# W_out's load moved to SyncE's queue, the temperature steps held until the first group's evictions, and a new set of planner ranks

## Chip, cores and metric

The kernel runs on one core of one Trainium2 chip. The metric is the device time of one execution in microseconds (us). The input is 32 sequences of 512 tokens with 256 features, all in f32.

## The reference, cut to what matters

Two blocks follow each other, each with a layer norm ahead of it and a residual sum behind it.

```
x = x + attention(layernorm(x))
    q     = tanh(x W_charge + b);  phi_c = mags * q^(0..4)
    shell = normalised(x W_shell + b);  phi_s = cos, sin(shell omega + bias)
    phi   = (phi_c outer phi_s) W_combine
    logits = phi phi^T * exp(-0.03 |i - j|) / (softplus(log_temp) + 0.1), causal
    out   = softmax(logits) (x W_v + b_v) W_out + b_out
x = x + slots(layernorm(x))
    route = gelu([x, slot mean] w1 + b1) w2 + b2, divided by (|tau| + 0.1)
    alpha = softmax over the 8 largest of 64, zero elsewhere
    gi    = alpha^T x / sum(alpha);  h = GRU(gi, slot state)
    out   = alpha (h wv + bv) wo + bo
```

## The kernel before, in words

The 32 sequences are worked on in 16 groups of two (group g from 0 to 15). A group goes through these stages, named by the tiles that TensorE (PE) writes:

- `pta` (first two groups): x is transposed on PE and copied to `xT` by ScalarE (ACT). Later groups load x a second time in blocks (`xb`, by SyncE's queue, SP) and transpose them on VectorE (DVE).
- `pf` (L959, eight tiles a group): x times the joined weights `wf`. DVE evicts each tile to `sv` (L972), with the layer norm applied. It needs `lna`, which GpSimd (POOL) makes from DVE's `bna` statistics.
- `ptq` (L1018) and `pts` (L1089): the charges (`qrep`, by POOL) and the shells (`shn`, by DVE) turned. ACT follows with `qs` and `shT`. `pp` (L1106) then gives the angles; ACT, DVE (`turn`), ACT's Sin and DVE's products make `tp`.
- `pph` (L1164): `tp` times W_combine. DVE multiplies it by the decays `dec_q` and `dec_k` into `phi` (L1179).
- `pl` (L1221): logits. DVE masks them and takes the lowest (`lg`, L1250), ACT takes the exponential (`pr`, L1262). `ptp` (L1299) turns the weights, ACT copies them (`prT`, L1317), `po` (L1305) multiplies by the values in `sv`, and DVE adds to x (L1334).
- second norm, then `xm` goes to DRAM and back (`xd`, `xmb`) and is transposed by DVE; in the last two groups PE does it (`ptb`).
- `ph` (L1431), `prr`, `prt`: the router; DVE takes the eight largest (`top`). `psi` (L1543), `pt_gi`, `prz`, `pn`, `pt_hn`, `pv`, `py` (L1704): the slots, the GRU and the way back. The result is stored by SP.

Weights are prepared once. `value_and_out` is called twice: for W_v and W_out (pair 0) and for wv and wo (pair 1). It loads the first matrix, the second, a bias `bv` and a bias `bo`, each on the queue that `engs` names; DVE centres the first matrix (pair 0 only, L432 to L435) and spreads `bv` over a tile (`spread`, L469); PE multiplies them (`pw` L446, `pb` L478); DVE copies the products into `wf` or `wov`. In pair 0 the first matrix is loaded by SP, the second by ACT's queue, the biases by POOL's.

The softmax temperature is made in three steps: `scalars_1` on ACT (two Abs, two Exp, the second of which makes `dec_k`), `scalars_2` on DVE (`sa`, `tau`, `rtau`), an Ln on ACT with a table load of its own, and `scalars_3` on DVE, which scales `dec_q`. The four reciprocals of `decays` (L643) wait for the first group's eight evictions.

The order of the work is not written by hand. Every piece is a `Step` with an engine, a cost, the steps that it comes after, and the buffers that it uses. `Plan.order()` places one step after another: of those that could start earliest, the one with the lowest rank. A step without a rank of its own gets one:

```
at = (1.0 - LATE) * s.at + LATE * (longest - s.tail)
delay, late = DELAY[s.stage]
s.rank = s.g * STRIDE + at + delay + late * max(0, s.g - last + 3)
```

HOP is what a step on another engine adds in the plan, TABLE and SWITCH are added to the rank of a step that needs another ACT table or another tiling of PE. Each engine then runs its instructions strictly in the order in which they were placed, and SP issues its DMAs in that order too.

Of the kernel before, what the change touches and what calls it, by code (L numbers as in the profile page):

```python
# [11 lines left out]
AF = mybir.ActivationFunctionType  # L12
# [25 lines left out]
DECAY = 0.3 / 10.0  # L38
# [33 lines left out]
}  # L72


HOP = 0.21
TABLE = 1.28
SWITCH = 4.13
STRIDE = 29.1
LATE = 0.69

DELAY = {
    "setup": (0.0, 0.0),
    "load": (-39.8, 3.7),
    "tokens": (0.2, -3.0),
    "angles": (-18.5, -12.2),
    "phi": (8.4, 6.8),
    "weights": (14.1, -12.0),
    "values": (5.1, -15.9),
    "normal": (-0.8, 5.2),
    "router": (-1.4, -7.2),  # L90
    "taken": (1.6, -23.5),
    "gru": (16.3, 6.1),
    "given": (-12.8, -6.4),
}

SPARE = 3
# [22 lines left out]
class Plan:  # L119
# [8 lines left out]
    def add(  # L128
        self,
        eng,  # L130
        cost,
        emit,
        after=(),
        uses=(),
        table=None,
        land=0.0,
        rank=None,
        spare=0,
        split=None,
    ):  # L140
        s = Step(eng, cost, emit, [a for a in after if a], list(uses), rank, table, land)
        s.spare, s.split = spare, split
        s.g, s.stage = self.group, self.stage
        for u in s.uses:
            u.users += 1
        for a in s.after:
            a.next.append(s)
        s.waits = len(s.after)
        self.steps.append(s)
        return s  # L150
# [95 lines left out]
def block_kernel(ctx: ExitStack, tc: tile.TileContext, a: dict, out: bass.AP):  # L246
    nc = tc.nc
# [24 lines left out]
    add = plan.add  # L272
# [79 lines left out]
    dec_k = const("dec_k", [P, T])  # L352
# [29 lines left out]
    def make_ident():  # L382
# [20 lines left out]
        rank=-40.0,  # L403
# [9 lines left out]
    def value_and_out(wv_ap, bv_ap, wo_t_ap, bo_ap, w_dst, b_dst, n, centred, engs, rank):  # L413

        at = 2 * n
        wv = part(at, 0, [P, KD, D])
        wo_t = part(at, KD * D, [P, KD, D])
        bv_rep = part(at, 2 * KD * D, [P, KD, P])
        bo = part(at, 2 * KD * D + KD * P, [P, D])
        of = wv.of  # L420
        bv = const(f"bv{n}", [P, KD])
        mean = const(f"wv_mean{n}", [P, KD])
        land = 3.5 if centred else None
        l_wv = load(engs[0], wv, rows(wv_ap), 256, rank=rank, land=land)
        l_wo = load(engs[1], wo_t, rows(wo_t_ap), 256, rank=rank, land=land)
        l_bv = load(engs[2], bv, bv_ap.rearrange("(k p) -> p k", p=P), 8, rank=rank)
        l_bo = load(engs[2], bo, bo_ap.partition_broadcast(P), 128, rank=rank)
        last = l_wv
        if centred:

            def centre():
                nc.vector.tensor_reduce(mean, wv(), AX.X, ALU.add)  # L432
                nc.vector.tensor_scalar(mean, mean, 1.0 / D, None, ALU.mult)
                for k in range(KD):
                    nc.vector.tensor_scalar(  # L435
                        wv()[:, k, :], wv()[:, k, :], mean[:, k : k + 1], None, ALU.subtract
                    )

            last = add("DVE", 1.6, centre, [l_wv], of, rank=rank)
        done, made = [], []  # L440
        for m in range(KD):
            pw = bank(f"pw{n}_{m}")

            def project(m=m, pw=pw):
                for k in range(KD):
                    nc.tensor.matmul(  # L446
                        pw()[:, 0:D],
                        wv()[:, k, m * P : (m + 1) * P],
                        wo_t()[:, k, :],
                        start=(k == 0),  # L450
                        stop=(k == KD - 1),
                    )

            s = add("PE", 1.6, project, [last, l_wo], [pw] + of, rank=rank)
            made.append(s)
            done.append(
                add(
                    "DVE",
                    0.42,
                    lambda m=m, pw=pw: nc.vector.tensor_copy(w_dst[:, m, :], pw()[:, 0:D]),  # L460
                    [s],
                    [pw],
                    rank=rank,
                )
            )

        def spread():
            for k in range(KD):
                nc.vector.tensor_scalar(  # L469
                    bv_rep()[:, k, :], onesP, bv[:, k : k + 1], None, ALU.mult  # L470
                )

        s = add("DVE", 0.5, spread, [l_bv, s_ones], of, rank=rank)
        pb = bank(f"pb{n}")

        def project_bias():
            for k in range(KD):
                nc.tensor.matmul(  # L478
                    pb()[:, 0:D],
                    bv_rep()[:, k, :],  # L480
                    wo_t()[:, k, :],
                    start=(k == 0),
                    stop=(k == KD - 1),
                )

        s = add("PE", 1.6, project_bias, [s, l_wo], [pb] + of, rank=rank)
        done.append(
            add(
                "DVE",
                0.42,  # L490
                lambda: nc.vector.tensor_tensor(b_dst, pb()[:, 0:D], bo(), ALU.add),
                [s, l_bo],
                [pb] + of,
                rank=rank,
            )
        )
        return done, made
# [7 lines left out]
        bias_f[:, C_V:NF],  # L505
        0,
        True,
        ("SP", "ACT", "POOL"),
        -40.0,
    )  # L510
    l_bsh = [
# [15 lines left out]
    s = add("PE", 0.8, mean_shell, l_sh + [s_ones] + s_wv_pe, [pm], rank=-38.0)  # L527
# [5 lines left out]
    for q in range(P // SQ):  # L533
        for k in range(KD):
# [8 lines left out]
                    rank=2.0,  # L543
                    land=4.0,
# [7 lines left out]
    for bb in range(GB):  # L552
        r = slice(bb * SHELL, (bb + 1) * SHELL)
        for h in range(2):
# [14 lines left out]
                rank=-15.0,  # L569
                land=5.0,  # L570
# [20 lines left out]
    sa = const("sa", [P, 1])  # L591
# [4 lines left out]
    df = part(0, 2 * KD * D + KD * P + D, [P, T])  # L596
    l_lt = load("SP", lt, a["log_temp"].partition_broadcast(P), 1, rank=-12.0)
    l_tau = load("SP", tau, a["tau"].partition_broadcast(P), 1, rank=-12.0)
# [10 lines left out]
    s_df = add("DVE", 0.42, lambda: nc.vector.tensor_copy(df(), di()), [s_di], [di] + df.of, rank=4.0)  # L609
# [3 lines left out]
    def scalars_1():  # L613
        nc.scalar.activation(sa, lt, AF.Abs)
        nc.scalar.activation(tau, tau, AF.Abs)
        nc.scalar.activation(sa, sa, AF.Exp, scale=-1.0)
        nc.scalar.activation(dec_k, df(), AF.Exp, scale=DECAY)

    def scalars_2():
        nc.vector.tensor_scalar(sa, sa, 1.0, None, ALU.add)  # L620
# [6 lines left out]
        nc.vector.reciprocal(rtemp, sb)  # L627
        nc.vector.tensor_scalar(dec_q, dec_q, rtemp, -1.0, ALU.mult, ALU.mult)

    s = add("ACT", 1.4, scalars_1, [l_lt, l_tau, s_df], df.of, table="exp", rank=4.0)  # L630
    s_exp = s
    s = add("DVE", 0.6, scalars_2, [s], rank=5.0)
    s_tau = s
    s = add("ACT", 1.5, lambda: nc.scalar.activation(sa, sa, AF.Ln), [s], table="ln", rank=5.0)
    s_sb = s

    def decays(after):

        s_rec = [
            add(  # L640
                "DVE",
                0.85,
                lambda c=c: nc.vector.reciprocal(  # L643
                    dec_q[:, c * P : (c + 1) * P], dec_k[:, c * P : (c + 1) * P]
                ),
                [s_exp] + after,
                rank=9.0,
            )
            for c in range(NT)
        ]  # L650
        s_dec.append(add("DVE", 1.0, scalars_3, [s_sb] + s_rec, rank=10.0))

    s_dec = []


    def make_mask():
# [18 lines left out]
        rank=-5.0,  # L675
# [12 lines left out]
            rank=30.0,  # L688
# [28 lines left out]
    s = add("PE", 0.3, hs_transposed, [s_hs, s_ident], [pt_hs], rank=41.0)  # L717
# [10 lines left out]
    def mean_hidden():  # L728
# [5 lines left out]
    s = add("PE", 0.8, mean_hidden, [s_hst, l_w1s], [pb1] + w1s.of, rank=42.0)  # L734
# [6 lines left out]
        rank=42.0,  # L741
# [11 lines left out]
    for lo, n in ((0, 2 * D), (2 * D, D)):  # L753
# [26 lines left out]
        s = add("PE", 2 * n / 300.0, hidden, [s_hst, l_whh], [pg] + hs_t.of + whh.of, rank=70.0)  # L780
# [566 lines left out]
    def router(g, s_x, ln):  # L1347
# [6 lines left out]
        for tiles in ((0, 1), (2,), (3,)):  # L1354
            c = slice(tiles[0], tiles[-1] + 1)
            s = add(
                "POOL",
                0.25,
                lambda c=c: nc.gpsimd.tensor_scalar(  # L1359
                    ln()[:, 2, :, c], ln()[:, 0, :, c], -1.0 / D, None, ALU.mult  # L1360
                ),
                [s_x[bb * NT + i] for bb in range(GB) for i in tiles],
                [ln],
            )
# [59 lines left out]
        for bb in range(GB):  # L1424
# [10 lines left out]
            s = add("PE", 1.78, hidden, done + w1_done, [dst, ph, h_t])  # L1435
# [22 lines left out]
        def routes_turned():  # L1458
# [5 lines left out]
        s = add("PE", 1.01, route, s_h + [l_w2], h_ts + [prr, rl_t], split="128x64")  # L1464
        s = add(
            "ACT",
            0.6,
            lambda: nc.scalar.activation(rl_t(), prr(), AF.Identity, bias=b2),
            [s] + l_b2,
            [prr, rl_t],  # L1470
        )
        s = add("PE", 0.44, routes_turned, [s], [rl_t, prt, rl])
# [9 lines left out]
        for t in range(GT):  # L1482
# [17 lines left out]
        s = add(  # L1500
            "ACT",
            0.68,
            lambda: nc.scalar.activation(rl(), rl(), AF.Exp, scale=rtau),
            [s, s_tau],
            [rl],
            "exp",
        )
# [225 lines left out]
    for g in range(NG):  # L1733
# [10 lines left out]
        sv, s_sv, phi, s_phi = features(g)  # L1744
# [66 lines left out]
```

## Time and profile before

| what | us |
|---|---|
| runs of the kernel, three | 692.91, 693.23, 696.05 |
| median | 693.23 |
| the profiled execution's own time | 696.3 |
| its span, first to last instruction | 694.5 |
| PE busy in that span | 664.7 (96%) |
| DVE busy | 581.4 (84%) |
| ACT busy | 454.2 (65%) |
| POOL busy | 214.0 (31%) |
| first matmul starts | 10.78 |
| last matmul ends | 688.5 |

The three engines DVE, ACT and POOL work beside PE; a wait of theirs counts only where PE ends up waiting too. PE's busy time is the sum over its matmuls, and what is left of the span is PE's idle time at the start, between stages and behind the last matmul. The granted clock in the page's PEclk row is PE's own; where it is below full speed, the same matmul takes longer.

### The profile page before, as it was taken

What the parts mean: (1) busy time and instruction counts of PE and PEld (TensorE: products, weight loads), DVE (VectorE), ACT (ScalarE), POOL (GpSimd) and SP (SyncE); (2) the same over time, 40 slices, a digit from 0 to 9 for tenths busy, and PEclk for the clock granted to TensorE, in tenths of its full rate; (3) what the DMA queues carried; (4) which work ended last, traced back from release to release, by engine and by line L of the source; (5) the groups of instructions that cost most, each with busy time, mean ns of one, the idle gap of its engine ahead of it and who ended that gap; (6) DMA issues with size and microseconds to landing.
All of it is one profiled execution on the core that took longest, in us unless ns stands there. A gap on an engine that the chain in (4) does not pass through costs nothing.

```text
span 694.5 us, 12285 instructions
## 1 busy us (share of the span) xinstructions
PE 664.7 (96%) x3946; PEld 457.7 (66%) x3946; DVE 581.4 (84%) x1812; ACT 454.2 (65%) x1064; POOL 214.0 (31%) x400
## 2 busy tenths in 40 slices
PE   3979999999999999999999999999999999999885
PEld 3747666667666666767666666666766676678453
DVE  3987878799898989989897988989898968878586
ACT  1446676848585866758495775758676677486731
POOL 3550524133150613324061422406151233212200
PEclk9999999999999999999999999999999999999989
DMA  6672732445544444444535353543543433301004
GB/s 179 165 204 68 205 100 73 111 141 130 154 115 130 150 114 161 101 143 128 175 93 149 125 122 135 139 152 96 148 132 82 161 82 87 97 1 62 0 13 170
DMA packets 174255, 83.25 MB, mean 120 GB/s; under 512 B 123664, under 2 KB 173392, under 8 KB 174192
## 3 DMA queue, kind: packets, MB, share of 16 engines
q1 hardware_dynamic: 172880, 81.95, 41.8%
q8 instruction: 31, 0.51, 0.3%
q10 hardware_dynamic: 1104, 0.36, 0.2%
q0 software_dynamic: 208, 0.17, 0.2%
q14 instruction: 32, 0.26, 0.1%
HBM read 50.67 MB, written 31.46 MB: 118 GB/s over the span
## 4 chain that ended last, share of the span: by engine, by line
PE 89%; DVE 4%; DMA 2%; ACT 2%; issue 1%; POOL 0%; ACTq 0%; DVEq 0%; SPq 0%
PE po L1305 20%; PE pf L959 19%; PE ph L1431 7%; PE pl L1221 5%; PE pph L1164 5%; PE ptp L1299 5%; PE psi L1543 5%; PE py L1704 4%; PE prz L1596 4%; PE pn L1596 2%; PE pv L1684 2%; PE prr L1454 2%; PE pta L1667 1%; PE pp L1106 1%; DMA setup<-in_W_out_t_dram 1%; DMA wih<-in_gru_wih_t_dram 1%
## 5 line engine op out<-in xcount | busy, mean ns | idle before, releaser
L1305 PE MATMUL po<-sv,prT 128*128 128x256 f32 x640 | 151.7, 381 | 0.8 <-ACT prT L1317 0.8
L1305 PEld LDWEIGHTS po<-sv,prT 128*128 128x128 f32 x640 | 115.5, 189 | 24.2 <-issue 8.6
L959 PE MATMUL pf<-wfb,xT 128*128 128x321 f32 x448 | 125.6, 436 | 0.0
L959 PEld LDWEIGHTS pf<-wfb,xT 128*128 128x128 f32 x448 | 83.5, 189 | 39.7 <-DVE top L1485 3.5
L1371 ACT ACTIVATE xm<-x,lnb 128x256 f32<-128x256 f32 x128 | 63.9, 502 | 61.7 <-POOL lnb L1359 61.6
L1359 POOL TENSOR_SCALAR lnb<-lnb 128x2 f32<-128x2 f32 (+1 forms) x48 | 20.8, 434 | 266.7 <-DVE x L1334 264.4
L1334 DVE SCALAR_TENSOR_TENSOR x<-po,den,x 128x256 f32<-128x256 f32 x128 | 57.9, 479 | 27.1 <-PE po L1305 26.6
L1262 ACT ACTIVATE pr<-lg,nm 128x512 f32<-128x512 f32 (+3 forms) x128 | 70.8, 557 | 4.9 <-DVE nm L1250 4.0
L972 DVE SCALAR_TENSOR_TENSOR sv<-pf,lna,bias_f 128x321 f32<-128x321 f32 x128 | 64.7, 537 | 5.7 <-PE pf L959 5.1
L1401 ACT ACTIVATE xm<-x,lnb 128x256 f32<-128x256 f32 x112 | 56.9, 589 | 7.8 <-POOL lnb L1387 7.8
L1250 DVE CUSTOM_DVE_ANT_0 lg<-pl,mask 128x512 f32<-128x512 f32 (+3 forms) x128 | 55.6, 479 | 1.6 <-PE pl L1221 1.3
L1718 DVE TENSOR_TENSOR x<-py,x 128x512 f32<-128x512 f32 x64 | 39.8, 683 | 17.4 <-PE py L1704 17.3
L1431 PE MATMUL ph<-xmT,w1b 128*128 128x512 f32 x112 | 52.7, 594 | 0.0
L1317 ACT COPY prT<-ptp 128x384 f32<-128x384 f32 (+1 forms) x96 | 46.1, 516 | 5.4 <-PE ptp L1299 5.2
L800 DVE BATCH_NORM_STATS2 bna<-x 128x6 f32<-128x256 f32 x128 | 49.4, 413 | 0.0
L1299 PE MATMUL ptp<-ident,pr 128*128 128x128 f32 x320 | 45.8, 275 | 0.0
L1221 PE MATMUL pl<-phi 64*128 64x256 f32 (+1 forms) x384 | 43.8, 358 | 0.2 <-DVE phi L1179 0.2
L1299 PEld LDWEIGHTS ptp<-ident,pr 128*128 128x128 f32 x320 | 36.5, 141 | 9.3 <-issue 6.8
L1164 PE MATMUL pph<-tp,wc 64*64 64x256 f32 x640 | 39.8, 392 | 0.8 <-DVE tp L1152 0.8
L1152 DVE TENSOR_TENSOR tp<-tp,qs 128x1024 f32<-128x1024 f32 x32 | 38.7, 1211 | 2.1 <-ACT tp L1138 1.9
L1221 PEld LDWEIGHTS pl<-phi 64*128 64x128 f32 x384 | 30.5, 186 | 11.1 <-issue 7.2
L929 DVE STREAM_TRANSPOSE xT<-xb 128x512 f32<-128x512 f32 x56 | 36.6, 685 | 0.0
(174 smaller groups left out, 1241.6 us busy)
## 6 DMA issues: line engine op xcount, KB each, us to landing
x<-in_x_dram SPq DMA_DIRECT2D x32, 512.0 KB, 4.6
out_dram<-x SPq DMA_DIRECT2D x64, 256.0 KB, 2.5
xb<-in_x_dram SPq DMA_DIRECT2D x112, 128.0 KB, 2.8
xd<-xm SPq DMA_DIRECT2D x28, 512.0 KB, 2.9
xmb<-xd SPq DMA_DIRECT2D x112, 128.0 KB, 2.7
setup<-in_gru_whh_t_dram SPq DMA_DIRECT2D x1, 768.0 KB, 4.6
wih<-in_gru_wih_t_dram SPq DMA_DIRECT2D x1, 768.0 KB, 10.6
wfb<-wf SPq DMA_DIRECT2D x8, 40.1 KB, 3.4
```

What stands on the lines that cost most here:

```text
L959: nc.tensor.matmul(pf()[:, 0:NF], tile_()[:, k, c * P : (c + 1) * P], w[:, k, :], start=(k == 0), stop=(k == KD - 1),)
L972: lambda t=t, pf=pf: nc.vector.scalar_tensor_tensor(sv()[:, t, :], pf()[:, 0:NF], ln()[:, 1, t : t + 1], bias_f, ALU.mult, ALU.add,),
L1164: nc.tensor.matmul(phs[h]()[bb * COMB : (bb + 1) * COMB, 0:HT], wc[r, m, :], tp()[r, m, bb * HT : (bb + 1) * HT], start=(m == 0), stop=(m ...
L1221: nc.tensor.matmul(pls[bb]()[:, off[i] + lo : off[i] + lo + w], phi()[r, 0, q : q + P], phi()[r, 1, k : k + w], start=True, stop=True,)
L1250: nc.vector.tensor_tensor_reduce(out=lg()[:, c], in0=pls[bb]()[:, c], in1=mask[:, T - w : T], scale=1.0, scalar=TOP, op0=ALU.add, op1=ALU.min,
L1262: nc.scalar.activation(pr()[:, c], lg()[:, c], AF.Exp, bias=nm(), scale=-1.0, accum_out=den()[:, tiles.index(i), bb : bb + 1],)
L1299: nc.tensor.transpose(pt()[:, j : j + P], prs[bb]()[:, j : j + P], ident)
L1305: nc.tensor.matmul(po()[:, d * D : (d + 1) * D], pr_t()[:, lo : lo + P], sv()[:, bb * NT + j, C_V:NF], start=(j == 0), stop=(j == i),)
L1334: nc.vector.scalar_tensor_tensor(xt()[:, t, :], po()[:, d * D : (d + 1) * D], den()[:, d, bb : bb + 1], xt()[:, t, :], ALU.mult, ALU.add, ...
L1371: lambda bb=bb, i=i: nc.scalar.activation(xm()[:, bb * NT + i, 0:D], xt()[:, bb * NT + i, :], AF.Square, bias=ln()[:, 2, bb, i : i + 1], a ...
L1401: nc.scalar.activation(xm()[:, t, 0:D], xt()[:, t, :], AF.Identity, bias=bias, scale=scale)
L1431: nc.tensor.matmul(ph(), w1[:, k, :], dst()[:, k, :], start=(k == 0), stop=(k == KD - 1))
```

## The change

- In pair 0, W_out is loaded by SP, directly behind W_v, and no longer by ACT's queue.
- The Exp that makes `dec_k` becomes a step of its own and keeps the early rank. The rest of `scalars_1`, `scalars_2` and the Ln move into `decays`, behind the first group's eight evictions, with rank 10.
- Router exponentials wait for `s_tau`, which is now that later `scalars_2`.
- HOP, SWITCH, STRIDE, LATE and all the stages' DELAY values have new numbers, and the landing time that the plan takes for pair 0 goes from 3.5 to 3.3.

```diff
-HOP = 0.21
+HOP = 0.32
 TABLE = 1.28
-SWITCH = 4.13
-STRIDE = 29.1
-LATE = 0.69
+SWITCH = 1.26
+STRIDE = 22.69
+LATE = 0.44
 DELAY = {
...
-    "load": (-39.8, 3.7),
-    "tokens": (0.2, -3.0),
-    "angles": (-18.5, -12.2),
-    "phi": (8.4, 6.8),
-    "weights": (14.1, -12.0),
-    "values": (5.1, -15.9),
-    "normal": (-0.8, 5.2),
-    "router": (-1.4, -7.2),
-    "taken": (1.6, -23.5),
-    "gru": (16.3, 6.1),
-    "given": (-12.8, -6.4),
+    "load": (33.2, -0.9),
+    "tokens": (7.9, -3.6),
+    "angles": (-12.9, -7.1),
+    "phi": (-3.7, -15.2),
+    "weights": (-20.3, -0.8),
+    "values": (14.8, 0.8),
+    "normal": (5.3, -1.0),
+    "router": (28.2, 13.5),
+    "taken": (-23.9, 11.4),
+    "gru": (-10.4, -13.6),
+    "given": (-16.6, -2.1),
 }
...
-        land = 3.5 if centred else None
+        land = 3.3 if centred else None
...
-        ("SP", "ACT", "POOL"),
+        ("SP", "SP", "POOL"),
...
         nc.scalar.activation(sa, sa, AF.Exp, scale=-1.0)
-        nc.scalar.activation(dec_k, df(), AF.Exp, scale=DECAY)
...
-    s = add("ACT", 1.4, scalars_1, [l_lt, l_tau, s_df], df.of, table="exp", rank=4.0)
-    s_exp = s
-    s = add("DVE", 0.6, scalars_2, [s], rank=5.0)
-    s_tau = s
-    s = add("ACT", 1.5, lambda: nc.scalar.activation(sa, sa, AF.Ln), [s], table="ln", rank=5.0)
-    s_sb = s
+    s_exp = add(
+        "ACT", 0.7,
+        lambda: nc.scalar.activation(dec_k, df(), AF.Exp, scale=DECAY),
+        [s_df], df.of, table="exp", rank=4.0,
+    )
 
     def decays(after):
...
-        s_dec.append(add("DVE", 1.0, scalars_3, [s_sb] + s_rec, rank=10.0))
-
-    s_dec = []
+        s = add("ACT", 0.7, scalars_1, [l_lt, l_tau] + after, table="exp", rank=10.0)
+        s = add("DVE", 0.6, scalars_2, [s], rank=10.0)
+        s_tau.append(s)
+        s = add("ACT", 0.3, lambda: nc.scalar.activation(sa, sa, AF.Ln), [s], table="ln", rank=10.0)
+        s_dec.append(add("DVE", 1.0, scalars_3, [s] + s_rec, rank=10.0))
+
+    s_dec, s_tau = [], []
...
-            [s, s_tau],
+            [s] + s_tau,
```

More of the change, by code (lines that the diff above doesn't have):

```diff
@@ L628, in scalars_3 @@
         nc.vector.tensor_scalar(dec_q, dec_q, rtemp, -1.0, ALU.mult, ALU.mult)
-    s = add("ACT", 1.4, scalars_1, [l_lt, l_tau, s_df], df.of, table="exp", rank=4.0)
-    s_exp = s
-    s = add("DVE", 0.6, scalars_2, [s], rank=5.0)
-    s_tau = s
-    s = add("ACT", 1.5, lambda: nc.scalar.activation(sa, sa, AF.Ln), [s], table="ln", rank=5.0)
-    s_sb = s
+    s_exp = add(
+        "ACT",
+        0.7,
+        lambda: nc.scalar.activation(dec_k, df(), AF.Exp, scale=DECAY),
+        [s_df],
+        df.of,
+        table="exp",
+        rank=4.0,
+    )
     def decays(after):
```

## The prediction, made before the changed kernel ran

> **What bounds the kernel now.** I read the page first, then PE's waits, then sums over stretches, then the timeline of the first 60 us and of the last 55. The page says that PE is the engine to look at:
>
> ```profile
> span 694.5 us, 12285 instructions
> PE 664.7 (96%) x3946; PEld 457.7 (66%) x3946; DVE 581.4 (84%) x1812; ACT 454.2 (65%) x1064; POOL 214.0 (31%) x400
> PE   3979999999999999999999999999999999999885
> PEclk9999999999999999999999999999999999999989
> ```
>
> PE is full but for both ends. The sums over stretches sharpen that: between 120 and 600 us it has no gap (busy 480.00 of 480.00), in the last stretch of matmuls it has 6 us of gaps and a lower clock.
>
> ```profile
> 120.00:600.00 480.00, 480.00 (x2883) 330.08 (x2882) 421.48 (x1310) 336.13 (x791) 157.39 (x281) 1.00 0.46 129
> 640.90:688.60 47.70, 41.48 (x199) 23.83 (x197) 33.14 (x108) 21.79 (x45) 3.96 (x6) 0.93 0.13 44
> ```
>
> In the middle a group takes 39.9 us of PE (first `psi` of one group to that of the next, 275.5 to 315.4). The change removes no matmul, and both programs have the same 1275 rows of matmuls with 204 changes of tiling against 205, so only PE's idle time and clock can differ. PE's waits, all the large ones:
>
> ```profile
> PE pw L446 <- DMA setup<-in_W_out_t_dram: 10.8, 1, 10.8
> PE ptq L1018 <- POOL qrep L998: 3.5, 2, 2.6
> PE prt L1460 <- ACT rlT L1468: 2.2, 1, 2.2
> PE pts L1089 <- DVE shn L1073: 1.3, 2, 0.9
> PE po L1305 <- ACT prT L1317: 0.8, 2, 0.4
> PE pl L1221 <- DVE phi L1179: 0.2, 1, 0.2
> ```
>
> First matmuls wait 10.8 us for W_out; later waits are small. For the first 60 us the timeline gives what the walk below uses:
>
> ```profile
> 5.27 1.10 DVE L435 TENSOR_SCALAR setup<-setup,wv_mean 128x256 f32<-128x256 f32 x2
> 38.36 0.43 SPq L280 DMA_DIRECT2D wih<-in_gru_wih_t_dram  x1
> 50.11 0.69 DVE L1250 CUSTOM_DVE_ANT_0 lg<-pl,mask 128x512 f32<-128x512 f32 x1
> 57.27 0.45 DVE L469 TENSOR_SCALAR setup<-onesP,bv 128x128 f32<-128x128 f32 x2
> ```
>
> W_v is centred by 6.37; DVE starts the first group's masking at 50.11, and spreads the second pair's `bv` only at 57.27, behind that masking.
>
> **Term 1, W_out behind W_v: PE starts 4.2 us earlier.** W_v lands at 4.28 and the first x half (512 KB, directly behind it) at 6.45, so 256 KB behind W_v take about 1.1 us: an estimate of 5.4. The centring (6.37) then ends last, and `pw` starts at 6.5 instead of 10.78. Bounds: 0, if ACT's queue was not what held W_out, to 4.4. The price on SP is one more issue of 0.5 us ahead of everything there; on ACT's queue b_shell and b_charge move up by 0.5.
>
> [...] The row of 8.9 us for W_out beside 3.5 for W_v of the same size speaks for position in the queue, and I take the row.
>
> **Term 2, the temperature steps: back 1.3.** The early Ln with its table load (1.28 and 0.20 on ACT at 19.7) goes, and nobody on PE waited for it. In the new order of ACT the three small activations (0.24, 0.22, 0.20) stand behind the first of the second group's four `xT` copies and ahead of the other three, and they wait for all eight evictions. Those now end near 24.0: the `lna` chain starts once x's second half is in statistics, about 14.7, and takes 3.2 on POOL (18.04 to 21.25 before), then eight evictions with four statistics between, six us as before. `xT`'s second copy ends at 25.5 instead of 24.2, so the second group's `pf` starts at 25.5 (before: 28.30). Bounds 0 to 1.5. The later Ln with its load stands on ACT between `qs` and `shT`, where ACT was idle for 2.49; it costs nothing, and if that cover were gone 1.5.
>
> **Term 3, the fill: back 4.8.** The lead is 2.6 when the second group's last `pf` ends (36.2 for 38.8). Then the new order puts `pt_hs`, `pb` and the 512-wide `pgh` ahead of the first group's `pph`. `pt_hs` needs the slot scales, the last of which was issued at 35.09 and takes 2.3: with the extra issue on SP, 37.9, and DVE gets to scale them at 40.1, behind three statistics, `turn`, an eviction and two more statistics (0.37 each, 1.1, 0.5). So PE idles from 36.2 to about 40.6, waits again for `mean_t` (42.4), and DVE's products of `tp` start at 42.4, where they started at 42.12. That the idle time holds new work (`pgh` 1.7 and 0.9, `pb` 0.6) is the gain left here.
>
> The next wait is the one that decides. On SP, wv, wo, `bv` and `bo` now stand directly behind wih, ahead of the blocks of x, and on DVE the spread of that `bv` (L469) stands ahead of the first group's `lg`. wih lands at 38.36 + 10.6 = 49.0, or 49.3 with the extra issue. 512 KB behind it at x's rate (512 KB in 2.2 us) land at 51.5, `bv` at 51.7. Then the spread (0.45) and `gh_n` (0.6) come, and `lg` starts at 52.8 instead of 50.11. On ACT the eight `pr` (0.75 each) and two `ang` stand ahead of the first `prT`, so the first `po` starts near 60.9. PE's work done by then is that of before at 57.3 plus 1.7 (`pw` twice, `pb` and the narrow `pgh`, 0.87 each, less the `po` of 1.73 that before had done). Before had done as much at 59.0. So the kernel is 1.9 behind there, and term 3 is 1.9 + 4.2 - 1.3 = 4.8. Bounds: 1.5 (`bv` lands beside wih) to 7.
>
> **Term 4, the groups in the middle: 0.** I compared, pair by pair in PE's order, the work between a matmul that starts a chain and the one that ends it. Most distances grow: `pl` to the first `ptp` from 2.8 to 12 us, last `po` to `ph` from 26.5 to 40. Some shrink: `pp` to `pph` from 16.8 to 9.6, `pph` to `pl` from 8.6 to 2.6, `pt_hn` to `pv` from 2.0 to 1.2. The rows of before show where waiting began: 0.18 at `pl` with 2.0 between, 0.43 at `po` with 0.8, none at `pv` with 0.9. Below these lie `po` of group 2 (0.9: no more than 0.3), `pv` and `py` of group 5 (0.5 each) and `pv` of group 13 (0.3): 1.6 in all, and before's waits of 0.94, 0.43 and 0.89 between 80 and 117 go: -0.7. The tight `pph` to `pl` may add as much, since four `phi` products (0.41 each) stand in DVE's queue. I take 0. Bounds: -2.3, all waits gone, to +10, one us in ten groups. Seven more table loads on ACT (58 for 51, 1.28 each) are 9 us spread over an engine that idles 11.8 in 40.
>
> **Term 5, the tail: -2.5.** Before, the last `po` ends at 640.9 and PE has 37.3 us of work left; the chain of the last group (norm, router, GRU) needs 53.6 to the end of the span. In the new order 42.8 us are left: groups 12 and 13 are later by a `psi`, a `py` pair, a `pv` and three turns (1.89 + 1.93 + 0.87 + 0.88). So the last `po` ends 5.5 earlier. The gaps behind it, 6.2 us, can take some of this: by the same chain, step by step, I get 56.7 from the last `po` to the end, 3 more than before. Bounds: -5.5 to +2.
>
> That 56.7 holds `psi` at full speed. Before, a gap of 2.23 ahead of `prt` is followed by the clock's fall, and the `psi` at 662.26 took 3.70 instead of 1.96. [...] The price of the gap near 38 is, by the row, some 1.7, and the wait for `bv` covers it.
>
> **Sum.** -4.2 + 1.3 + 4.8 + 0 - 2.5 = -0.6 on the profiled execution: span 693.9, own time 695.7 for 696.3. The median of the three runs (693.23) is 3.1 below the profiled execution; so 692.6 against that median. A difference of 0.5% (3.5 us) is about what a measurement of this kernel can tell from none.
>
> **Rivals.**
> *The middle waits (slower).* With 2.6 between `pph` and `pl`, PE waits each time that VectorE's queue is over 0.5 us behind; VectorE is busy 35.5 of 40 us, so it has little to catch up with. Against it: PE never waited for VectorE between 120 and 600, and work that comes late also gives the queue time. One us in each of ten groups gives 692.6 + 10 = 703; from 0.4 a group on it is slower by over 0.5%. Chance 0.30.
> *The fill keeps the lead (faster).* If `bv` lands by 50 and the slot scales are early, term 3 is 1.5 instead of 4.8, and a tail at -5 gives 692.6 - 3.3 - 2.5 = 686.8. For it: DVE idles before 42, and the tail has 6 us of gaps. Against: wih's row of 10.6 us. Chance 0.30.
> *W_out lands no earlier.* Then PE starts at 10.7, but the fill still waits for the same wih and `bv`: the lead is lost here instead of there, and the time is about 694. Chance 0.08, and it counts as no change, like the forecast with 0.32.
>
> So faster 0.30, same 0.40, slower 0.30. Each unlikely end beyond 685.5 and 701.5 gets 0.1: the range holds the faster rival with a point to spare and most of the slower one. The likeliest case's own range is 689.5 to 696.5.
>
> **What the new profile would show.** Term 1: the first `pw` at 6.5, waiting for DVE's centring. Term 2: ACT's `tau` at 24, between two `xT` copies. Term 3: a PE gap over 4 us near 38, DVE waiting for `bv` before the first `lg`, the first `po` near 61. Term 4: PE busy over 99% between 120 and 600. Term 5: the last `po` some 6 us earlier, 56 to 57 us before the end. The forecast is wrong if PE's waits for `phi` or `prT` add up to over 4 us, or if the first `po` stands before 58.

## The result, and the profile after

| | before | after |
|---|---|---|
| median of the runs made side by side, us | 694.64 | 700.89 |
| lowest to highest | 692.91 to 698.51 | 699.72 to 704.6 |
| the profiled execution, its own time | 696.3 | 699.72 |
| its span | 694.5 | 697.9 |

The ratio is 1.0085, with a 95% interval of 1.0065 to 1.0106. The change makes the kernel slower by 0.85%, more than the 0.5% that the prediction took as the least that can be told from no change; the forecast was 0.1% faster. By the medians the change costs 6.2 us, while the spans of the two profiled executions differ by 3.4: the one of before is 1.7 us above its median, the one of the changed kernel 1.2 below. What follows accounts for those 3.4 us, and says where other executions of the same order differ. The page of the changed kernel, in the rows that were shown of before:

```profile
span 697.9 us, 12280 instructions
...
PE 667.4 (96%) x3946; PEld 456.8 (65%) x3946; DVE 588.2 (84%) x1812; ACT 458.8 (66%) x1071; POOL 203.1 (29%) x400
...
PE   6979999999999999999999999999999999999885
...
PEclk9989999999999999999999999999999999999989
```

The first slice of PE rises from 3 to 6: the start has moved. A new 8 stands in the third slice of the clock: the clock is at half speed there for 6.8 us, in before for 3.4 us (from 42.8). The sums over the same two stretches as before:

```profile
120.00:600.00 480.00, 478.46 (x2873) 327.50 (x2871) 421.82 (x1288) 342.22 (x797) 147.99 (x281) 1.00 0.45 125
640.90:688.60 47.70, 40.04 (x184) 22.48 (x183) 33.58 (x104) 22.08 (x48) 3.56 (x5) 0.93 0.14 48
```

The middle has 1.5 us of gaps where it had none. PE's waits, the large ones (total, times, longest):

```profile
PE pw L446 <- DVE setup L435: 6.0, 1, 6.0
PE pt_hs L721 <- DVE hs L714: 3.6, 1, 3.6
PE prt L1466 <- ACT rlT L1474: 3.3, 1, 3.3
PE pv L1690 <- ACT hnT L1581: 2.4, 3, 1.2
PE po L1311 <- ACT prT L1323: 1.8, 2, 1.0
PE py L1710 <- DVE val L1698: 1.3, 3, 0.5
```

`pw` waits 4.8 us less, and for the centring instead of W_out; the 3.5 us of `ptq` for `qrep` are gone too. The wait for `hs` is new, and those for `rlT`, `hnT` and `prT` were shorter before (2.2, 1.0 and 0.8). The one for `val` was 1.2: the prediction's list, said to hold all the large waits, leaves out five of before between 0.6 and 1.2 us (at `py`, `pv`, `psi`, `pph` and `prz`). The page's DMA part and the timeline of the fill (DVE, SP and PE, in order of time):

```profile
wih<-in_gru_wih_t_dram SPq DMA_DIRECT2D x1, 768.0 KB, 8.9
```
```profile
37.23 0.43 SPq L280 DMA_DIRECT2D wih<-in_gru_wih_t_dram  x1
...
38.11 0.69 PE L721 MATMUL pt_hs<-ident,hs 128*128 128x128 f32 x2 [3.58 <-DVE hs L714]
...
48.58 0.48 DVE L469 TENSOR_SCALAR setup<-onesP,bv 128x128 f32<-128x128 f32 x2 [0.53 <-DMA bv<-in_bv_dram]
...
49.64 0.68 DVE L1256 CUSTOM_DVE_ANT_0 lg<-pl,mask 128x512 f32<-128x512 f32 x1
...
56.34 2.00 PE L1311 MATMUL po<-sv,prT 128*128 128x256 f32 x8 [0.80 <-ACT prT L1323]
```

`wih` is issued 1.1 us earlier than before (38.36), not later, and `lg` starts half a microsecond earlier than before (50.11). This is one execution: in two other kernels below with the same order up to there, `wih` was issued at 38.8 and 39.0.

To see where a lead is won and lost, I weigh every matmul with the mean time that its form takes from start to start in the middle of before, and compare the times at which two traces have done the same amount. The **lead** over before, in us, at before's own times:

| before's time | 22.8 | 52.1 | 100.7 | 172.0 | 322.4 | 422.3 | 612.0 | 642.6 | 682.6 | end of span |
|---|---|---|---|---|---|---|---|---|---|---|
| after | 5.2 | 3.4 | 2.7 | 4.2 | 3.1 | 1.0 | 0.3 | -0.8 | -3.3 | -3.4 |
| both edits, old ranks | 4.8 | 4.1 | 4.2 | 4.2 | 4.2 | 4.2 | 4.2 | 4.2 | 4.8 | 4.8 |
| new ranks alone | 0.6 | -0.8 | -1.6 | 0.0 | -1.1 | -3.3 | -3.9 | -4.9 | -8.0 | -8.1 |

Each row is one trace against one trace, and executions of the same order differ by some 2 us, nearly all of it before 100 us: the first `po` stands at 56.34 here and at 58.57 in the kernel with the short additions told below, and a later `pph` at 251.42 and 253.64. The second and third row are experiments, told below. The changed kernel starts with a lead of 5.2 us, loses 1.0 of it by 172 us, 3.9 between there and 612 us, and 3.7 behind that.

### The profile page after: what moved, and what is told of

Read it like the earlier page. It is cut to its first block, busy times and chain, and to the rows that moved or that the text cites. A ratio compares the mean times of both kernels' runs of the same rounds, so it can differ in the third digit from the quotient of the medians.

```text
span 697.9 us, 12280 instructions
## 1 busy us (share of the span) xinstructions
PE 667.4 (96%) x3946; PEld 456.8 (65%) x3946; DVE 588.2 (84%) x1812; ACT 458.8 (66%) x1071; POOL 203.1 (29%) x400
## 4 chain that ended last, share of the span: by engine, by line
PE 81%; DVE 6%; ACT 5%; DMA 3%; SPq 2%; POOL 1%; issue 1%; DVEq 0%; ACTq 0%
PE po L1311 20%; PE pf L965 16%; PE ph L1437 7%; PE pph L1170 5%; PE pl L1227 5%; PE ptp L1305 5%; PE py L1710 4%; PE psi L1549 4%; PE prz L1602 3%; DMA x<-in_x_dram 2%; PE prr L1460 2%; PE pv L1690 2%; SPq L280 2%; PE pn L1602 2%; ACT pr L1268 2%; ACT xm L1407 1%
## 5 line engine op out<-in xcount | busy, mean ns | idle before, releaser
L1311 PE MATMUL po<-sv,prT 128*128 128x256 f32 x640 | 148.6, 380 | 2.0 <-ACT prT L1323 1.8
L965 PE MATMUL pf<-wfb,xT 128*128 128x321 f32 x448 | 131.4, 438 | 0.0
L978 DVE SCALAR_TENSOR_TENSOR sv<-pf,lna,bias_f 128x321 f32<-128x321 f32 x128 | 66.6, 541 | 17.5 <-PE pf L965 12.2
L1268 ACT ACTIVATE pr<-lg,nm 128x256 f32<-128x256 f32 (+3 forms) x128 | 70.5, 552 | 5.8 <-DVE nm L1256 4.0
L1256 DVE CUSTOM_DVE_ANT_0 lg<-pl,mask 128x512 f32<-128x512 f32 (+3 forms) x128 | 56.2, 485 | 10.4 <-PE pl L1227 9.5
L1340 DVE SCALAR_TENSOR_TENSOR x<-po,den,x 128x256 f32<-128x256 f32 x128 | 55.4, 473 | 10.5 <-PE po L1311 10.3
L1365 POOL TENSOR_SCALAR lnb<-lnb 128x2 f32<-128x2 f32 (+1 forms) x48 | 14.5, 303 | 126.9 <-DVE x L1340 126.7
L1525 POOL TENSOR_TENSOR al<-rl,asum 128x512 f32<-128x512 f32 x14 | 14.6, 1045 | 114.6 <-DVE asum L1518 114.6
L806 DVE BATCH_NORM_STATS2 bna<-x 128x6 f32<-128x256 f32 x128 | 45.8, 413 | 2.3 <-DMA x<-in_x_dram 2.3
L1305 PEld LDWEIGHTS ptp<-ident,pr 128*128 128x128 f32 x320 | 36.5, 140 | 12.1 <-issue 6.6
L1051 POOL TENSOR_TENSOR sq<-sv 128x256 f32<-128x256 f32 x32 | 19.9, 622 | 81.2 <-DVE sv L978 77.1
L1158 DVE TENSOR_TENSOR tp<-tp,qs 128x1024 f32<-128x1024 f32 x32 | 40.4, 1264 | 1.3 <-ACT tp L1144 1.0
```

Of the source, the lines that this page charges most:

```text
L965: nc.tensor.matmul(pf()[:, 0:NF], tile_()[:, k, c * P : (c + 1) * P], w[:, k, :], start=(k == 0), stop=(k == KD - 1),)
L978: lambda t=t, pf=pf: nc.vector.scalar_tensor_tensor(sv()[:, t, :], pf()[:, 0:NF], ln()[:, 1, t : t + 1], bias_f, ALU.mult, ALU.add,),
L1256: nc.vector.tensor_tensor_reduce(out=lg()[:, c], in0=pls[bb]()[:, c], in1=mask[:, T - w : T], scale=1.0, scalar=TOP, op0=ALU.add, op1=ALU.min,
L1268: nc.scalar.activation(pr()[:, c], lg()[:, c], AF.Exp, bias=nm(), scale=-1.0, accum_out=den()[:, tiles.index(i), bb : bb + 1],)
L1305: nc.tensor.transpose(pt()[:, j : j + P], prs[bb]()[:, j : j + P], ident)
L1311: nc.tensor.matmul(po()[:, d * D : (d + 1) * D], pr_t()[:, lo : lo + P], sv()[:, bb * NT + j, C_V:NF], start=(j == 0), stop=(j == i),)
```

## Experiments: which part of the change

The change has three parts: W_out's queue, the temperature steps, and the new ranks. All ratios below are to the kernel before.

**Both edits with the old ranks** (the changed kernel; HOP, SWITCH, STRIDE, LATE and DELAY as before):

> The changed kernel with the old planner numbers (HOP, SWITCH, STRIDE, LATE, DELAY), so W_out and the temperature steps alone. Its order behind the last `po` is that of before. Theory A (the new ranks cost the time, in the middle and in the tail; the other two edits gain): PE starts at 6.0 instead of 10.8 us, keeps 2 to 4 us of this lead to the end, ratio to before 0.994 to 0.997. Rival B (the lead is lost in the fill, and the moved temperature steps hold ScalarE): ratio 1.000 or above.

Measured: 691.68 us, 0.9947 [0.9926, 0.9967]. It beats both kernels. Its lead in the table is constant from 50 us to the tail, and its middle is full again:

```profile
120.00:600.00 480.00, 480.00 (x2876) 328.61 (x2875) 421.60 (x1304) 335.74 (x788) 157.39 (x281) 1.00 0.45 128
```

**The new ranks alone** (the kernel before with the new numbers):

> Before with the new planner numbers alone; W_out stays on ScalarE's queue and the temperature steps stay early. Its order behind the last `po` is that of the changed kernel. Theory A: slower than the changed kernel by the lead of W_out, 2 to 4 us, so 1.012 to 1.015 of before, and some 62 us from the last `po` to the end. Rival B: faster than the changed kernel, 1.000 to 1.004.

Measured: 704.52 us, 1.0131 [1.0109, 1.0152]. So the new ranks cost 1.3% and the two edits give 0.5%; added up that is 0.8%, the measured 0.85%.

**Each edit alone, with the old ranks.** W_out's queue:

```diff
-        land = 3.5 if centred else None
+        land = 3.3 if centred else None
...
-        ("SP", "ACT", "POOL"),
+        ("SP", "SP", "POOL"),
```

> Before with W_out behind W_v on SyncE's queue (and the plan's landing of 3.3) alone, old planner numbers. The planner makes another order of the later groups from it, with a `py` pair more behind the last `po`. Theory A: PE starts at 6.0, the lead at the first `po` is 2 to 4 us; the end depends on the order behind the last `po`, and loses 1 us of it for the extra `py` additions: ratio 0.995 to 0.999. Rival B: 1.000 or above, as the lead is gone at the first `po`.

And the other one, the temperature steps as in the change with W_out left on ACT's queue:

> Before with the temperature steps behind the first group's evictions alone, W_out on ScalarE's queue, old planner numbers. Theory A: PE starts at 10.8 as before, and the steps neither gain nor lose more than 1 us at the first `po`: ratio 0.999 to 1.003, what there is coming from the other order of the last groups (as in the kernel with W_out alone, a `py` pair more behind the last `po`). Rival B: the small activations ahead of three `xT` copies hold PE for 1 us or more, and the ratio is above 1.003.

Measured: 756.02 us, 1.0871 [1.0845, 1.0897], and 754.97 us, 1.0870 [1.0841, 1.0899]. The rivals' "or above" covers the numbers, but neither theory had the reason. W_out alone starts PE at 6.0 and leads by 5.1 us at the first `po`, more than theory A's 2 to 4, but it is 10 us behind at 172 us and 59 at the end of the span. PE's largest wait and the middle of the kernel with W_out alone:

```profile
PE ptp L1299 <- ACT pr L1262: 17.8, 6, 8.8
```
```profile
120.00:600.00 480.00, 447.17 (x2601) 304.06 (x2600) 384.70 (x1194) 312.45 (x719) 129.78 (x249) 0.96 0.41 116
```

The planner places the steps in another order here, without the period of 240 matmuls that PE's order has in before, and from 121 us on PE's order is the same in both kernels. The edits don't cost 8.7%: the order that the planner falls into does. A part can only be priced with the placed order held.

**W_out's queue with the order held.** The kernel with both edits and old ranks, in its own order; only the issuing engine differs:

```diff
+        if centred:
+            l_wo.emit = lambda: nc.scalar.dma_start(out=wo_t(), in_=rows(wo_t_ap))
```

> The kernel with both edits and the old ranks, its whole placed order kept instruction by instruction, but W_out's DMA is issued by ScalarE as before the change (it is the only difference, so the order of the later groups cannot tip). Theory A (the 4.2 us earlier start of TensorE is W_out's alone, and the temperature steps cost nothing where they now stand): the start goes back to about 10.8, the lead to 0 to 0.5 us, and the time to 0.999 to 1.001 of the kernel before. Theory B (a good part of the gain came from the temperature steps, ScalarE and VectorE being free of them in the fill): it keeps 1 us or more, 0.995 to 0.9985.

Measured: 695.25 us, 1.0008 [0.9994, 1.0022], and PE's first wait is that of before:

```profile
PE pw L448 <- DMA setup<-in_W_out_t_dram: 10.7, 1, 10.7
```

So W_out's queue is worth the whole 0.6% (0.9947 against 1.0008, some 4.2 us): theory A. The temperature steps, which this kernel still has in their new place, gain nothing; the interval leaves room for a cost of up to 1.5 us. The trace has a place for 0.7 of it, as a `ptq` of the second group waits 3.23 us for `qrep` where before it waited 2.56, but no run shows that the steps are the cause. The run changes the issuer and the place among the transfers together, so what each of them is worth is not shown. On ACT's queue, in before, W_out was issued at 1.78, behind two halves of x (1.23 and 1.73 on SP's), and landed at 10.64; on SP's, in the changed kernel, at 1.23, ahead of them (1.72 and 2.24), and landed at 5.34.

## Experiments: where the new ranks cost

For these the kernel is planned twice, with the old and the new numbers, and one order is followed up to a planned time, the other for all that is left:

```diff
...
-        for s in plan.order():
+        then = plan.order(OLD)
+        head = [s for s in plan.order(NEW) if s.start < CUT]
+        taken = set(head)
+        for s in head + [s for s in then if s not in taken]:
             s.emit()
```

**The fill.** Old ranks to 55 us, new ones behind:

> The changed kernel, with the steps that the planner starts in its first 55 us placed by the old ranks and everything later by the new ones; on TensorE only instruction rows 22 to 84 of 1275 move against the changed kernel (hs' transposes, the mean, the hidden-state product go back behind the first group). Theory A (the new ranks' order of the fill costs time for good: gap of 3.6 us and half clock until 43.8): the gap is gone and 1.5 to 2 us are back at the end, 698.9 to 699.4 where the changed kernel has 700.9, ratio 1.005 to 1.007. Rival (the lead lost in the fill was regained by 122 us in the changed kernel, 4.0 against 4.16, because work was waiting there; what the fill gives is lost by the second group): the end does not move by more than 0.5 us, ratio 1.0075 to 1.0095.

Measured: 701.21 us, 1.0093 [1.0071, 1.0115]; the number is the rival's. But the run does not take out what it was meant to: the gap at `pt_hs` is gone, another of nearly the same length stands in its place, and the clock's third slice (35.0 to 52.4 us) is an 8 all the same, as in the changed kernel.

```profile
PEclk9989999999999999999999999999999999999989
```
```profile
PE ptq L1040 <- POOL qrep L1020: 3.2, 1, 3.2
```

What a gap and half clock there cost stays untested by it.

The converse, new ranks to 55 us and old ones behind:

> Both edits; the steps that the planner starts in its first 55 us placed by the new ranks, everything later by the old ones. With it the parts of the new ranks can be added up. Theory A (the fill's gap of 3.6 us and its half clock cost nothing in the end with the new ranks behind them, since the new order regains it by 122 us, but the old order has nothing there to regain it with): 1 to 2 us later than with the old ranks throughout, 692.7 to 693.7, ratio 0.996 to 0.998. Rival (what the fill loses is regained behind any order, as the second group's transfers wait anyway): 0.994 to 0.9955.

Measured: 695.65 us, 0.9996 [0.9982, 1.0010], by the ratios 3.4 us more than with old ranks throughout, by the medians and the leads 4.0; theory A named the direction and half the size. Its lead is 4.6 at 22.8 us and 0.2 from 100 us to 640 us. So ahead of the old order the fill of the new ranks does lose some 4 us, and the old order keeps what it is handed, a lead or a loss, all through the middle; the new order's middle does not.

**The middle.** That is what these two runs and the table say of it together: with the new order the lead falls by 3.9 us between 172 and 612 us in the changed kernel, by 3.9 with the ranks alone, and by 3.9 behind the old fill (3.8 to -0.1); with the old order, by 0.0 behind either fill. The order of the middle costs 3.9 us, whatever it starts from (4.2, 0.0 or 3.8). In the trace of after, 1.5 us of this are waits: 1.16 at `pv` (351.6 to 352.8), where `hnT` stands in ACT's queue behind two normalisations (`xm`, 1.08), 0.23 at the `py` behind it, and 0.15 at a `po`. The other 2.4 us are in no gap of the list. Between 160 and 600 us PE changes its tiling 147 times instead of 140, and a 128x128 matmul ahead of such a change takes 202 ns to the next start instead of 109 (medians of before in that stretch, 23 and 421 matmuls): about 0.7 us, an estimate. The rest stays open.

**The tail, first try.** New ranks to 560 us, old ones behind:

> The changed kernel, with everything that the planner starts after its 560 us placed by the old ranks: on TensorE rows 0 to 1058 of 1275 are the changed kernel's, the last 208 those of the kernel with both edits and old ranks; VectorE's from row 1000 on. Theory A (the new ranks' order of the tail costs the last 3.6 us, by VectorE's queue in front of the last group's chain): PE reaches the tail with a lead of 0.3 us over before and keeps it, 1.000 to 1.003 of before, 696 to 697 us where the changed kernel has 700.9. Rival (the tail is late because of what stands before it, whatever its order): 1.006 to 1.010.

Measured: 709.04 us, 1.0212 [1.0188, 1.0236], outside both theories. The seam itself made a wait:

```profile
PE pta L1689 <- POOL al L1541: 9.3, 1, 9.3
```

It is paid before 572 us, so the time says nothing on the tail of the changed kernel. The trace does: at equal work this kernel is 12.1 us behind at 612 us and 11.7 at the end, so its tail in the old order loses nothing. In the other traces the old order's tail, from 612 us to the end, loses nothing either (gains of 0.6 with both edits and behind the new fill), while the new one loses 3.7 in the changed kernel, 4.2 with the ranks alone and 4.5 behind the old fill. The tail is slow by its order, not by what stands before it.

**Is it VectorE's time?** The additions of groups 12 and 13 made short, everything else as in the changed kernel; it leaves out the other 248 of each 256 columns of these two groups:

```diff
+                    w = D if g not in (12, 13) else 8
-                    y = xt()[:, t : t + 2, :]
+                    y = xt()[:, t : t + 2, 0:w]
...
-                        y, py().rearrange("p (j d) -> p j d", d=D), y, ALU.add
+                        y, py().rearrange("p (j d) -> p j d", d=D)[:, :, 0:w], y, ALU.add
```

> The changed kernel in its own order, but the eight VectorE additions of the slots' values to x in groups 12 and 13 add 8 of each 256 columns (the other columns of those two groups are left out of the output); TensorE's work, every wait and every DMA stay. VectorE gets 8 x about 0.5 = 4 us shorter, 2 us of it ahead of the last group's normalised tokens, 2 us ahead of its last weights. Theory A (VectorE's queue sets the tail): the end comes 2 to 4 us earlier, 697 to 699, ratio 1.003 to 1.006. Rival (TensorE's work behind the last po, 42.8 us, and its clock set it): no more than 0.7 us, ratio 1.0075 or more.

Measured: 700.19 us, 1.0079 [1.0057, 1.0100]. That is the rival's number, and the traces agree. First the changed kernel's, then this one's, DVE and PE at the end:

```profile
667.62 2.37 PE L1549 MATMUL psi<-xm,al 128*64 128x257 f32 x16
...
671.08 2.48 DVE L1724 TENSOR_TENSOR x<-py,x 128x512 f32<-128x512 f32 x4 [0.24 <-PE py L1710]
...
675.99 0.63 PE L1673 MATMUL pta<-ident,al 128*128 128x128 f32 x4 [0.40 <-DVE al L1525]
676.55 1.96 PE L1549 MATMUL psi<-xm,al 128*64 128x257 f32 x16
```
```profile
669.84 3.03 PE L1549 MATMUL psi<-xm,al 128*64 128x257 f32 x16
...
674.83 0.26 DVE L1725 TENSOR_TENSOR x<-py,x 128x16 f32<-128x16 f32 x2 [0.61 <-PE py L1710]
...
678.32 0.60 PE L1673 MATMUL pta<-ident,al 128*128 128x128 f32 x4
678.85 1.96 PE L1549 MATMUL psi<-xm,al 128*64 128x257 f32 x16
```

The additions shrink to 0.26 for two and wait for `py` instead, and PE no longer waits for `al`; still, from group 14's `psi` to the last group's there are 9.0 us, in the changed kernel 8.9. PE itself has `py` of group 13, `pt_gi`, `prz` and `pn` to do in between.

**Is it the order of group 13's last pieces?** Both edits, new ranks to 650 us, old ones behind. On PE this moves `psi` of group 14, its gates and the last `psi` ahead of group 13's `pt_hn`, `pta`, `pv` and `py`, and group 14's `prt` ahead of four `ptb`; ACT's and DVE's lists change with it.

> The changed kernel, with only the steps that the planner starts after its 650 us placed by the old ranks. On TensorE rows 0 to 1227 of 1275 stay; behind the last prt, group 14's psi, its gates and then the last group's psi come ahead of group 13's slot update (pt_hn, pta, pv, eight py), which the new ranks put ahead of them; VectorE's list changes from row 1177, ScalarE's from 571, GpSimd's and SyncE's not at all. Theory A (the tail's loss is that order: group 13's pieces stand ahead of the last group's psi on TensorE, and their waits for hn ahead of it on VectorE): the lead stays where it is at 660 us, about -0.9 us of before, and the end comes 2 to 3 us earlier than the changed kernel's, 698 to 699, ratio 1.004 to 1.0065. Rival (the tail is late already at 640 to 655 us, by group 12's py and the second die of that order, and nothing behind 660 matters): less than 1 us, ratio 1.0070 to 1.0095.

Measured: 698.57 us, 1.0041 [1.0025, 1.0057], 2.3 us less than the changed kernel by the medians, 3.1 by the ratios. The converse, old ranks to 650 us and new ones behind:

> The converse: the kernel with both edits and the old ranks, with only the steps that the planner starts after its 650 us placed by the new ranks, so that group 13's pt_hn, pta, pv and py stand ahead of the last two psi on TensorE (rows 0 to 1234 stay). Theory A: 2 to 3 us later than with the old ranks throughout (691.7), 693.7 to 694.7, ratio 0.9975 to 0.9995. Rival: no more than 1 us later, ratio 0.994 to 0.9965.

Measured: 694.98 us, 0.9984 [0.9967, 1.0000], 3.3 us more than with old ranks throughout by the medians, 2.6 by the ratios. Both fall where theory A put them. PE's timeline from the last `prt` to the last `psi`, of the changed kernel and then of the one with `psi` first:

```profile
662.34 1.11 PE L1466 MATMUL prt<-ident,rlT 128*128 128x128 f32 x4 [3.26 <-ACT rlT L1474]
664.29 0.66 PE L1573 MATMUL pt_hn<-ident,hn 128*128 128x128 f32 x2 [0.83 <-DVE hn L1663]
...
665.77 1.92 PE L1690 MATMUL pv<-wov,hnT 128*128 128x256 f32 x4
...
669.91 2.00 PE L1710 MATMUL py<-val,alT 64*128 64x256 f32 x16
```
```profile
663.46 0.66 PE L1482 MATMUL prt<-ident,rlT 128*128 128x128 f32 x4 [2.33 <-ACT rlT L1490]
665.39 3.33 PE L1565 MATMUL psi<-xm,al 128*64 128x257 f32 x16 [1.27 <-DVE top L1507]
...
674.52 1.96 PE L1565 MATMUL psi<-xm,al 128*64 128x257 f32 x16 [0.28 <-DVE al L1541]
```

In the changed kernel three pieces of group 13 come between `prt` and the first `psi`, and its `py` between the two `psi`: 14.2 us from `prt` to the last `psi` (676.55), against 11.1. The wait ahead of `prt` differs too, 3.26 against 2.33, and it is 3.25 in the converse: ACT makes the last `rlT` behind group 14's exponential, whose table load waits longer for DVE's `rl` in the new order. Before and after:

```profile
657.69 1.28 ACT L1503 ACT_TABLE_LOAD   x1 [0.41 <-DVE rl L1494]
```
```profile
659.70 1.28 ACT L1509 ACT_TABLE_LOAD   x1 [1.43 <-DVE rl L1500]
```

In the converse PE's list is the old one up to this `prt`, so there the longer wait, by 1.0 us, is made by ACT's and DVE's order; the rest of the price lies between `prt` and the last `psi`. No run moves PE's list alone.

**A version that might be faster still.** In the kernel with both edits and old ranks, group 13's new state, `pt_hn`, `hnT` and `pv` are moved into PE's wait ahead of the last `prt`:

```diff
...
+        ahead(a["new_state"], b["sums"])
+        (turned,) = a["hnT"].after
+        ahead(turned, c["prt"])
+        ahead(a["hnT"], c["prt"])
+        ahead(a["pv"], b["psi"])
```

> A version that may beat the kernel with both edits and the old ranks (691.7): in its placed order four steps of group 13 are moved into TensorE's last long wait (2.2 us for the last rlT, after which the clock is at half for 6.8 us). VectorE makes group 13's new state ahead of group 14's sums, where it waits 2.1 us for ScalarE anyway; TensorE's pt_hn goes ahead of the last prt, pv ahead of group 14's psi, ScalarE's copy of hnT behind the last rlT. Theory A (the wait is cut into pieces under 1.5 us, the clock stays full, psi takes 2.0 in place of 3.7 us): 1 to 2.5 us earlier, 689 to 690.7, ratio 0.991 to 0.9935. Rival (the chain through the exponential and the maxima on VectorE sets the last weights, wherever group 13's pieces stand, or the moved new state itself waits for GpSimd and holds the sums up): 0.994 to 0.997.

Measured: 692.06 us, 0.9939 [0.9918, 0.9960], no difference from 691.68 that can be told. PE in the last part:

```profile
655.77 0.41 PE L1575 MATMUL pt_hn<-ident,hn 128*128 128x128 f32 x2 [1.23 <-DVE hn L1665]
656.76 0.94 PE L1466 MATMUL prt<-ident,rlT 128*128 128x128 f32 x4 [0.59 <-ACT rlT L1474]
657.50 1.92 PE L1694 MATMUL pv<-wov,hnT 128*128 128x256 f32 x4
...
667.62 1.96 PE L1550 MATMUL psi<-xm,al 128*64 128x257 f32 x16 [1.43 <-DVE al L1526]
```

The wait is cut into 1.23 and 0.59, as meant, but the clock falls all the same (0.50 from 657.0 to 660.4 us, as long as in the kernel that it was made from, which has it from 658.8 to 662.2 and not for the 6.8 us of before; `pv` takes 1.92 instead of 1.03), and what PE has won it waits for at the end, for `al` on DVE. The rival holds: there the chain through the exponential and the maxima sets the last `psi`.

## Why the prediction was wrong

Each term beside what the lead of after shows (minus is a gain):

| term | predicted | measured | where it is read |
|---|---|---|---|
| 1 W_out, 2 temperatures | -4.2, +1.3 | -5.2 together | lead at 22.8 us |
| 3 the fill | +4.8 | +1.0 (1.2 to 2.5 in three other kernels of the same order) | lead 5.2 to 4.2 at 172 us |
| 4 the middle | 0 | +3.9 | 4.2 to 0.3 at 612 us |
| 5 the tail | -2.5 | +3.7 | 0.3 to -3.4 at the end |
| sum | -0.6 | +3.4 | spans 694.5 and 697.9 |

**Term 1 was right.** W_out landed at 5.34 (forecast 5.4), `pw` started at 6.0 behind the centring (6.5), and with the order held the queue alone is worth 4.2 us.

**Term 2 had the wrong place.** The three activations stand at 22.4 on ACT, earlier than the 24 that I had worked out from the eight evictions, and the second group's `pf` starts at 23.07, not 25.5. The lead is still 5.2 at 30 us. The run with the order held allows 0 to 1.5 us, and 0.7 at most is seen, at a `ptq`, where the prediction had none of it.

**Term 3 had the right gap and the wrong wait.** The gap at `pt_hs` is there (3.58 us; forecast 36.2 to 40.6, found 34.5 to 38.1), and so is the half clock, 6.8 us of it where before had 3.4. But the wait said to decide, for `bv`, is not: I had `bv` landing at 51.7, by `wih`'s 10.6 us behind an SP queue half a microsecond later. SP was 1.1 us earlier and `wih` took 8.9, so DVE waited 0.53 us for `bv` and the first `po` came at 56.3 instead of 60.9 (the prediction's own sign of being wrong was one before 58). SP's earlier issue belongs to this execution: with the new ranks to 560 us, to 650 us and with the short additions, all of the same order up to there, `wih` was issued at 37.6, 39.0 and 38.8, and the first `po` came at 56.8, 58.4 and 58.6. But `wih` took 8.5 in the second of these too. The landing time had been carried over from before, where the transfers stand in another order. By 100 us the fill had lost 2.5, and 1.5 of that came back by 172 us. The run with the new fill and the old rest shows that the same fill costs some 4 where the order behind it regains nothing: its price depends on what follows it.

**Term 4 was mis-sized: 0, measured 3.9**, inside its own bounds of -2.3 to +10. Of the pairs named, `pv` and `py` of group 5 waited (1.16 and 0.23, forecast 0.5 each), and `po` of group 2 did not: what stood between the two matmuls of a pair was counted, but not ACT's queue between them. The gains set against them, before's three waits between 80 and 117 us (2.26), came only in part, as after has 1.44 of waits there (0.39 at a `ptq`, 1.05 at the first `po` of group 1); the table counts them in the row of term 3. Of the 3.9, 1.5 are waits and some 0.7 changes of tiling, by the estimate above; the cause of the rest is open. PE was busy 99.7% between 120 and 600, which by the prediction's own sign would have shown the term right: a busy share hides 3.9 us in 480. The rival's wait, `pl` for `phi`, did not come; it is not among PE's waits over 0.5 us.

**Term 5 is the step that failed, by 6.2 us**, in the sentence "by the same chain, step by step, I get 56.7 from the last `po` to the end". The last `po` did end 5.95 us earlier (634.95 for 640.9). To the end it then took 62.96 us, not 56.7. PE's sums from the last `po` to the last `prt`, of before and then of after, say why:

```profile
640.90:660.33 19.43, 17.05 (x69) 8.64 (x68) 10.46 (x43) 14.91 (x30) 3.96 (x6) 1.00 0.00 0
```
```profile
634.95:662.34 27.39, 23.32 (x112) 12.81 (x111) 17.53 (x61) 18.19 (x40) 4.97 (x8) 0.99 0.11 39
```

The work that was moved behind the last `po` all stands ahead of the last `prt`: 23.32 us of PE for 17.05, 6.3 more. I had let the gaps in the tail take some of it, but the gaps lie behind that work, where they grew: here from 2.4 to 4.1 us, by the longer wait for `rlT` and one for `rw`. From `prt` to the last `psi` it is 14.2 us for 11.5, and the two runs that change the order at 650 us show that the new one costs 2.3 to 3.3 us from there on. From the last `psi` to the end it is 1.3 us less than before. That the order is the cause is shown by the old order's tails, which lose nothing; how the loss ahead of the last `prt` divides between PE's added work and the longer waits is read from the sums alone. My first cause after the result, DVE's additions, fell: shortening them gave nothing, and the order of group 13's pieces did.

**The clock.** The prediction read the clock's fall in before beside the gap of 2.23 us ahead of `prt`: it fell at 660.58, 0.25 us behind the end of that gap, and stood at 0.50 until 667.40. In the changed kernel it fell inside the gap of 3.58 us at `pt_hs`, 2.5 us after its start, and stood at 0.50 from 37.00 to 43.80:

```profile
37.00:43.80 6.80, 4.55 (x10) 2.32 (x10) 6.19 (x15) 0.34 (x1) 3.55 (x8) 0.50 1.02 315
```

In the version with waits of 1.23 and 0.59 us, 0.41 of work between them, it fell at 657.0, 2.5 us after the start of the first wait. How long a gap has to be for a fall is not shown.

## What to carry to other kernels

When work is moved behind the last big stage, ask for each piece whether it stands ahead of the final chain on its engine: a gap in the tail absorbs only work that is placed inside it. An edit to a kernel whose order a planner makes has two effects, its own and the planner's answer; price them apart by holding the placed order, since here the answer was worth anything from nothing to 8.7%. A lead won at the start reaches the end only behind an order that keeps it, so follow it at equal work through the whole trace, not by the busy share.

## What was not expected of the hardware

Splitting a wait did not keep the clock: the 2.2 us for `rlT`, cut into 1.23 and 0.59, was followed by the same fall to half speed, for 3.4 us with the one wait and with the two. The stretches at half clock that ended before the program did lasted 3.4 and 6.8 us in before, and 6.8 twice in the changed kernel. The same 256 KB of W_out landed at 5.34 us as the second transfer on SP's queue (the changed kernel) and at 10.64 on ACT's behind two of 1 and 64 KB (before). And `wih`, 768 KB, took 8.9 us from issue to landing in the changed kernel, 8.0 in the one with its fill and the old rest and 8.5 in the one with its order to 650 us, where it had taken 10.6 in before and, with the old order of the fill, 9.7 with both edits, 9.8 with W_out left on ACT's queue and 10.4 ahead of the new rest.
